# Two layers of cross-attention in float32: the projections of layer 0 in two column tiles of 64

## The chip, the cores and the metric

The kernel runs on one core of one Trainium2 chip. The metric is the device time of one execution in microseconds (us); of several runs the median is given. TensorE multiplies matrices and writes its results to PSUM, ScalarE and VectorE read PSUM and write SBUF, GpSimd works in SBUF, and SyncE issues most DMAs.

## The reference

The input x has 4 batches of 1024 rows of 512, the context 4 batches of 1024 rows of 384. Everything is float32. Layer 0 has 16 heads of 64, layer 1 has 16 heads of 32.

```python
def layer0(x, context):
    h = layernorm(x) * gamma + beta
    Q, K, V = h @ Wq, context @ Wk, context @ Wv          # 16 heads of 64: 1024 wide
    attn = softmax(Q K^T) * 64 ** -0.5                    # per head, 1024 x 1024
    return x + (attn V) @ Wo + bo

def layer1(x, context):
    xn = x * rsqrt(mean(x * x) + 1e-5) * norm_w
    q, (k, v) = xn @ wq, context @ wkv                    # 16 heads of 32: 512 wide
    q, k = normalised(rotated(q)), normalised(rotated(k)) # rotary, then length 1 per head
    attn = softmax(q k^T * sqrt(32))
    return x + (attn v) @ wout

out = layer1(layer0(x, context), context)
```

## The kernel before, in words

The work goes batch by batch; in each batch layer 0 comes first and layer 1 second. [...]

**Layer 0** works on pairs of heads (8 pairs of 2 x 64 = 128 features). The attention of a pair takes 8 steps, one for each 128 query rows (`Attention0.step`). A step does this:
- `scores` (L372): eight passes on TensorE, with 64 rows of the array for each of the two heads, so that two heads run side by side. The trace shows each float32 matmul as two passes.
- at every second step `factors_turned` (L440): two transposes of 128 x 128 (rT) bring the softmax's divisors to the layout of the product.
- VectorE takes each row's maximum (L395), ScalarE the exponential (L396), VectorE turns 32 x 32 squares over (L401), and at the end of every second step 16 DMAs (L407) put the squares of two steps where they belong (eT).
- part of the other work, up to 1.8 us by the program's own estimate, is issued behind the scores. The class `Units` keeps it as a list of small units with estimated costs, and `fill` issues units until the estimate is used up.
- at every second step `product` (L449), the product av with v: sixteen rounds of two column tiles of 64, one for each head.

The units of layer 0 are mostly projections: for the pair two ahead kT, qT and v (`project` and `values`, tiles pkT, pqT and pv), and the sums into x, which are the products with Wo of finished pairs (`add_units`, po, then added to x by VectorE at L301). Towards the end of layer 0 the first projections of layer 1 join them (`rotated_chains` and `value_chains`, k_p and pv from wkv), with transposes among them (L519, k_t). Between the layers there is a short stage with the last sums into x, the norm of layer 1 (transposes at L253), and the first q projections.

**Layer 1** works on blocks of four heads. Its scores (L597) use 32 rows of the array for each of four heads, and its products av (L636, L647) four column tiles of 32. The units there are projections of layer 1, sums into x, and the preparation of the next batch.

All projections and sums go through one helper, `matmul` (L158 is the call in it). It splits the columns of the stationary operand, that is the output's partitions, into `which["cols"]` column tiles and issues one matmul for each; the moving operand is the same for all of them. `which["cols"]` is read when a unit is issued. It is 1 at the start and in layer 0, 4 in layer 1, and is set back behind each batch's layer 1. Transposes do not go through the helper.

Of the kernel before, what the change touches and what calls it, by code (L numbers as in the profile page):

```python
# [107 lines left out]
def xattn_kernel(ctx: ExitStack, tc: tile.TileContext, a: dict, out: bass.AP):  # L108
# [10 lines left out]
    def score(name, shape=(P, S)):  # L119
        return ps_s.tile(list(shape), F32, tag="s", name=name)  # L120

    which = {"n": 0, "from": 0, "cols": 1}

    def bank(name):

# [13 lines left out]
    cols = const.tile([P, 3, NQ], F32, name="cols")  # L139
# [599 lines left out]
    for b in range(B):  # L739
# [6 lines left out]
        for p in range(NPAIR):  # L746
# [51 lines left out]
            for i in range(NT):  # L798
# [8 lines left out]
                n = NT * (NPAIR - p if later else 1) - i  # L807
# [41 lines left out]
        for half in range(2):  # L849
            n = 0  # L850
# [45 lines left out]
            kT, qT, v = kT1, qT1, att1.v1  # L896
        att1.finish()
        att1.quotient()
        which["from"], which["cols"] = 0, 1
        if b == B - 1:  # L900
            tail = flat(adds[1][6:])
        else:
# [42 lines left out]
```

## Time and profile before

| | |
|---|---|
| median of 3 runs | 2983.13 us (2977.34 to 2984.37) |
| profiled execution | 2979.04 us |
| its span, first to last instruction | 2976.8 us |
| granted TensorE clock | 0.997 |
| TensorE matmuls, weight loads | 2914.2 us busy, 1541.9 us busy |
| VectorE, ScalarE, GpSimd | 2228.5, 1429.5 and 416.5 us busy |

The profile is of one execution, so sums made from it are compared with that execution's time. Weight loads run beside matmuls on TensorE and are listed apart as PEld. In the groups of instructions a line gives the source line, engine, operation, the tiles written and read, the shape, the number of passes, the busy time, the mean time of one in ns, and the idle time of the engine before them with what ended it. The shape 128*64 means 128 rows and 64 columns of the array. The timeline gives the start, the length, and the number of passes of each stretch of equal instructions; the start of the next stretch tells how long the engine was taken, since the lengths shown include the time in which a result is still on its way. One batch takes about 737 us, of which 432 us lie between layer 0's first scores and its last.

### The profile page before, as it was taken

The numbers are of one execution on the slowest core, as the hardware profiler recorded it, in microseconds if no ns is written. First come the engines' busy times: TensorE is split into PE (matmuls) and PEld (weight loads), VectorE is DVE, ScalarE is ACT, GpSimd is POOL, SyncE is SP. The second block draws the span as 40 slices with busy tenths as digits, with TensorE's granted clock in tenths as the row PEclk, the third lists the DMA queues.
The fourth block names the chain that finished last, engine by engine and source line by source line (L and its number), as shares of the span: only waits on it lengthen the run. The fifth ranks groups of instructions, "written<-read, shape, count | busy, mean of one in ns | idle before, by whom it ended". The sixth has DMA issues, their size and how long they took to land.

```text
span 2976.8 us, 60525 instructions
## 1 busy us (share of the span) xinstructions
PE 2914.2 (98%) x24748; PEld 1541.9 (52%) x24748; DVE 2228.5 (75%) x2824; ACT 1429.5 (48%) x2265; POOL 416.5 (14%) x392
## 2 busy tenths in 40 slices
PE   8999999999999999999999999999999999999998
PEld 5544546555544555655554454555455455555544
DVE  4777795877777779587777777958767777795777
ACT  3444443656534444465644444446664444444664
POOL 0010012420000002232000000223100000023310
PEclk9999999999999999999999999999999999999999
DMA  5787674010388777301048887730104878772000
GB/s 146 169 197 180 158 178 114 21 35 25 74 200 196 183 161 178 95 21 35 25 95 213 183 177 169 166 84 21 35 25 117 209 176 182 167 171 66 2 2 30
DMA packets 177525, 348.49 MB, mean 117 GB/s; under 512 B 37600, under 2 KB 93152, under 8 KB 177248
## 3 DMA queue, kind: packets, MB, share of 16 engines
q1 hardware_dynamic: 175056, 343.43, 48.8%
q8 instruction: 196, 3.21, 0.5%
q10 hardware_dynamic: 2192, 1.19, 0.1%
q14 instruction: 81, 0.66, 0.1%
HBM read 67.64 MB, written 8.39 MB: 26 GB/s over the span
## 4 chain that ended last, share of the span: by engine, by line
PE 82%; DVE 8%; DMA 3%; SPq 3%; ACT 2%; issue 1%; POOL 1%; ACTq 0%; DVEq 0%
PE s L372 15%; PE av L449 13%; PE po L158 10%; PE s L597 7%; PE pv L158 7%; PE av L636 6%; PE pqT L158 6%; PE pkT L158 5%; PE q_p L158 3%; PE av L647 2%; SPq L407 2%; PE k_p L158 2%; DVE both L613 2%; DMA eT<-e 1%; PE rT L440 1%
## 5 line engine op out<-in xcount | busy, mean ns | idle before, releaser
L396 ACT ACTIVATE e<-s,m 128x1024 f32<-128x1024 f32 x512 | 565.6, 1109 | 666.7 <-DVE m L395 623.1
L395 DVE TENSOR_REDUCE m<-s 128x1 f32<-128x1024 f32 x512 | 602.6, 1218 | 321.4 <-PE s L372 321.4
L607 ACT ACTIVATE e<-s 128x1024 f32<-128x1024 f32 x512 | 496.5, 1022 | 315.3 <-PE s L597 300.2
L401 DVE STREAM_TRANSPOSE e<-e 128x1024 f32<-128x1024 f32 x512 | 606.6, 1223 | 46.9 <-ACT e L396 41.1
L372 PE MATMUL s<-qk 64*128 64x512 f32 x2048 | 520.5, 615 | 6.0 <-ACT e L396 5.3
L449 PE MATMUL av<-eT,v 128*64 128x256 f32 x4096 | 470.3, 382 | 7.8 <-DMA eT<-e 6.2
L613 DVE TENSOR_TENSOR both<-e 128x512 f32<-128x512 f32 x512 | 342.1, 699 | 128.9 <-ACT e L607 93.7
L449 PEld LDWEIGHTS av<-eT,v 128*64 128x64 f32 x4096 | 285.5, 137 | 205.3 <-issue 50.2
L372 PEld LDWEIGHTS s<-qk 64*128 64x128 f32 x2048 | 181.8, 186 | 262.6 <-issue 188.5
L597 PE MATMUL s<-q,k 32*128 32x256 f32 x4096 | 304.7, 401 | 5.8 <-ACT q L524 2.7
L597 PEld LDWEIGHTS s<-q,k 32*128 32x128 f32 x4096 | 190.8, 184 | 149.6 <-ACT e L607 71.4
L158 PE MATMUL po<-wo,vals 128*128 128x512 f32 x512 | 239.6, 601 | 2.5 <-ACT v L130 2.5
L158 PE MATMUL pqT<-hT,w 128*128 128x512 f32 (+1 forms) x800 | 241.3, 597 | 0.7 <-ACT hT L255 0.7
L441 ACT COPY vals<-rT 128x256 f32<-128x256 f32 x128 | 47.7, 372 | 327.4 <-PE rT L440 327.4
L301 DVE TENSOR_TENSOR x<-x,po 128x512 f32<-128x512 f32 x200 | 133.6, 678 | 82.6 <-PE po L158 82.6
L158 PEld LDWEIGHTS pv<-w,cT 128*128 128x128 f32 (+1 forms) x2400 | 176.7, 152 | 30.3 <-issue 27.2
L158 PE MATMUL pv<-w,cT 128*128 128x128 f32 (+1 forms) x2400 | 186.5, 275 | 0.0
L158 PE MATMUL pkT<-cT,w 128*128 128x512 f32 (+1 forms) x600 | 182.7, 601 | 1.0 <-ACT cT L130 1.0
L617 DVE TENSOR_TENSOR both<-both 128x1024 f32<-128x1024 f32 x128 | 159.7, 1248 | 4.4
L158 PEld LDWEIGHTS po<-wo,vals 128*128 128x128 f32 x512 | 90.9, 190 | 106.5 <-issue 102.3
L158 PEld LDWEIGHTS pqT<-hT,w 128*128 128x128 f32 (+1 forms) x800 | 85.9, 151 | 112.2 <-issue 105.9
L636 PE MATMUL av<-e,v 128*32 128x256 f32 x2048 | 137.0, 385 | 0.0
(461 smaller groups left out, 2669.9 us busy)
## 6 DMA issues: line engine op xcount, KB each, us to landing
eT<-e SPq DMA_DIRECT2D x2048, 128.0 KB, 2.4
xr<-in_x_dram SPq DMA_DIRECT2D x32, 256.0 KB, 4.0
x<-in_x_dram SPq DMA_DIRECT2D x32, 256.0 KB, 4.0
wo<-in_Wo_dram SPq DMA_DIRECT2D x16, 512.0 KB, 4.0
out_dram<-x SPq DMA_DIRECT2D x32, 256.0 KB, 2.7
w<-in_Wq_dram SPq DMA_DIRECT2D x31, 256.0 KB, 3.9
c<-in_ctx_dram SPq DMA_DIRECT2D x32, 192.0 KB, 3.8
wkv<-in_wkv_dram SPq DMA_DIRECT2D x16, 384.0 KB, 3.3
```

Source lines behind the costliest of these rows:

```text
L158: nc.tensor.matmul(o[rr], lhsT[:, rr], rhs, start=start, stop=stop)
L301: nc.vector.tensor_add(xt[t], xt[t], pp[0])
L372: nc.tensor.matmul(sc[j][:, kb * 512 : (kb + 1) * 512], pr["qT"][r[j], i * P : (i + 1) * P], pr["kT"][r[j], kb * 512 : (kb + 1) * 512], st ...
L395: nc.vector.tensor_reduce(m[:, j : j + 1], sc[j], AX.X, ALU.max, negate=True)
L396: nc.scalar.activation(e[j], sc[j].rearrange("p (g s) -> p g s", g=4), AF.Exp, bias=m[:, j : j + 1], accum_out=l[:, j : j + 1])
L401: nc.vector.transpose(e[j], e[j])
L449: nc.tensor.matmul(av[r[j], :W].rearrange("p (t a i) -> p t a i", t=BQ, a=4), pr["v"][:, k, r[j]], eT[:, j, :, :, k * 32 : (k + 1) * 32], ...
L597: nc.tensor.matmul(sc[j // 2][:, j % 2, c, :], kT[rr, g, k * P : (k + 1) * P], qT[rr, g, qb * WQ : (qb + 1) * WQ], start=True, stop=True,)
L607: nc.scalar.activation(e, sc[u], AF.Exp, scale=float(np.sqrt(np.float32(HD1))))
L613: nc.vector.tensor_add(self.both[:, kk, 2 * u : 2 * u + 2, :], es[u][:, :, 0, :], es[u][:, :, 1, :])
L617: nc.vector.tensor_add(self.both[:, 0], self.both[:, 0], self.both[:, kk])
L636: nc.tensor.matmul(self.av[rr, 0, :], v[g][:, 2 * kk + c, rr], es[j // 2][:, j % 2, c, :], start=first and c == 0, stop=end and c == 1,)
```

## The change

In layer 0 the helper splits every projection and every sum into x into two column tiles of 64, where it issued one matmul of 128 columns. In layer 1 it stays at four tiles. The order of the units, their estimated costs, the tiles, loads and evictions stay as they are.

```diff
@@ -119,7 +119,7 @@
-    which = {"n": 0, "from": 0, "cols": 1}
+    which = {"n": 0, "from": 0, "cols": 2}
@@ -896,7 +896,7 @@
         att1.finish()
         att1.quotient()
-        which["from"], which["cols"] = 0, 1
+        which["from"], which["cols"] = 0, 2
         if b == B - 1:
```

The helper itself is not edited:

```python
    def matmul(o, lhsT, rhs, start, stop):

        w = P // which["cols"]
        for j in range(which["cols"]):
            rr = slice(j * w, (j + 1) * w)
            nc.tensor.matmul(o[rr], lhsT[:, rr], rhs, start=start, stop=stop)
```

## The prediction

> **What bounds the kernel now.** I read the busy line first, then the groups of instructions by shape, then the timeline of TensorE alone, and last the starts of single matmuls in order.
>
> ```profile
> PE 2914.2 (98%) x24748; PEld 1541.9 (52%) x24748; DVE 2228.5 (75%) x2824; ACT 1429.5 (48%) x2265; POOL 416.5 (14%) x392
> ```
>
> TensorE is busy nearly all the time; no other engine comes near. Its groups by shape (stationary rows*columns; x counts passes, two to one f32 matmul):
>
> ```profile
> L449 PE MATMUL av<-eT,v 128*64 128x256 f32 x4096 | 470.3, 382 | 7.8 <-DMA eT<-e 6.2 <-DMA w<-in_Wq_dram 0.9 <-DMA x<-in_x_dram 0.7
> L158 PE MATMUL po<-wo,vals 128*128 128x512 f32 x512 | 239.6, 601 | 2.5 <-ACT v L130 2.5
> L158 PE MATMUL pqT<-hT,w 128*128 128x512 f32 x416 | 195.1, 601 | 0.0
> L158 PE MATMUL pv<-w,cT 128*128 128x128 f32 x1248 | 150.6, 277 | 0.0
> L158 PE MATMUL pv<-w,cT 128*32 128x128 f32 x1152 | 35.9, 273 | 0.0
> ```
>
> The 128*128 rows of L158 (3132 passes with the smaller ones) are what the change splits; the 128*32 row is the same work run in layer 1 in four column tiles. Idle time before these rows is a few us, so the length of layer 0 is the length of TensorE's own stream. Two steps of that stream, TensorE only:
>
> ```profile
> 1005.93 1.99 PE L372 MATMUL s<-qk 64*128 64x512 f32 x8
> 1007.85 0.44 PE L440 MATMUL rT<-ident,rb_(3, 3)_7795 128*128 128x128 f32 x2
> 1008.12 1.02 PE L158 MATMUL pkT<-cT,w 128*128 128x512 f32 x2
> 1009.07 3.67 PE L449 MATMUL av<-eT,v 128*64 128x256 f32 x32
> 1012.68 1.99 PE L372 MATMUL s<-qk 64*128 64x512 f32 x8
> 1014.60 2.84 PE L158 MATMUL pkT<-cT,w 128*128 128x512 f32 x6
> 1017.27 2.74 PE L158 MATMUL pqT<-hT,w 128*128 128x512 f32 x6
> ```
>
> Read start to start. A "round" is what runs side by side: one pass untiled, two passes of two tiles. The single starts give medians: a round of 512 takes 429 ns, of 256 takes 216, and both hold for 128*128, two tiles and four tiles alike. On top come two stalls wherever the shape of the tile changes:
> - at the boundary: 96 ns out of 128*128 (134 cases into scores, 106 into av), 103 out of 128*64, 99 out of 64*128, 117 out of 128*32;
> - in the first round after it, since the next load isn't ready: 107 ns into 128 columns, 54 into 64, 27 into 32 (58 for a 128-wide transpose[...]).
>
> So pkT x2 is 2 x 429 + 96 = 954 (0.95 read), av is 16 x 216 + 54 + 103 = 3613 (3.61), scores 4 x 429 + 107 + 99 = 1922 (1.92). Between transposes and untiled projections nothing is paid: rT takes 2 x 109 + 56.
>
> [...]
>
> **The change part by part.** Instruction order, loads, evictions, buffers and DMAs stay, so nothing is moved past a queue and no wait is added. What changes is the mode of L158 in layer 0, thus which boundaries pay. Counts are from the starts in order:
> 1. scores to projection, 124 times: 99 + 107 becomes 99 + 54, -53 each: -6.6 us. The boundary from 64*128 into 128*64 isn't in the trace; its neighbours are 99 (into 128*128) and 111 (32*128 into 128*32); I take 99, the other end adds 1.5.
> 2. projection to av, 106 times: 96 + 54 becomes 4, as between 128*32 projections and av in layer 1 (2 + 3): -146: -15.5 us.
> 3. av to projection, 5 times: 103 + 107 becomes 4: -1.0 us.
> 4. transpose to projection, 129 times (mostly rT, some k_t): 7 becomes 96 + 54, as the 22 times when rT goes straight to av: +143: +18.4 us.
> 5. projection to transpose, 19 times: 4 becomes 103 + 58: +3.0 us.
> 6. projection to scores, 134 times: 96 becomes 103: +0.9 us.
>
> Sum: -0.8 us. In the two steps above: with the transpose, scores to scores stays 6.75 us, for the switch only moves from behind the projection to ahead of it; in the other step 53 - 7 = 46 ns go. Odd-numbered steps are where something is won (123 x 46 ns = 5.7 us); transposes outside the pattern, in the stage between the layers and without av behind, give it back.
>
> 7. Rounds: 512 and 256 wide, nothing (429 and 216 in all tilings; 1 ns off would be 1 us). The 128-wide pv takes 111.7 ns a round untiled and 109.2 in four tiles; two tiles may be either: 1248 x 0 to 2.5 = 0 to -3.1 us. I take half, -1.5.
> 8. 3132 more passes and as many loads to issue: costed at nothing; streaming covers them. Four instructions a round of at least 109 ns are half of what the 128*32 pv issues in that time. If that cover goes, rival B.
>
> Total -2.3 us, of the profiled execution's 2979.04 us (span 2976.8, 2.2 around it). The median of the three runs, 2983.13, stands 4.1 above it, so on that footing 2980.8, say 2981. Nothing downstream must keep up: VectorE is at 75%, and TensorE's waits that remain in layer 0 (single ones of 0.4 to 1.8 us, mostly av waiting for eT) may swallow a few us of the 5.7 or be shortened by the switch that now lies ahead of them; I allow 3 us each way.
>
> **Rivals.**
> A, the forecast: stalls move and cancel, 2981, between 2976 and 2987 with the ends above. For it: every price but those of items 1 and 7 is read at the same shapes in this trace. Summing these prices and the single waits gives back the whole TensorE stream, 2968 us from first to last start, within 3 us.
>
> B, slower: two 64-column loads behind each other don't hide. av shows 54 in the round after a switch, but with 256-wide rounds and another moving operand for each tile. If a projection pays 107, as one 128-column load does, items 1 and 4 lose 53 in 253 places, 13.4 us: 2994, +0.4%. It decides from some 94 ns on. Instruction supply gives the same sign: 6264 more instructions are 24 blocks of the instruction queue's 16 KiB (196 packets now, 1.06 us median); were each waited for whole, 26 us: 3007. Against: four tiles pay 27, one load, not 107; and layer 1 runs 8 instructions in 216 ns. But in layer 0 the DMA engines are far busier.
>
> C, faster: the transposes cost less beside 64-column tiles than item 4 says, since the weight loads of the projection behind are already in when the two rT are done. All of item 4 gone would be -18.4: 2962. Half of it: 2972. Against: the 22 cases of rT to av pay 96 + 54 without exception. Or the waits for eT shrink: they hold about 8 us in front of av, so at most 2973.
>
> D: the change doesn't act, because a unit queued in layer 0 runs in layer 1. That is so already for the 128*32 rows, since the width is read when a unit is issued; the 3132 passes counted are those issued under the old width of one. I leave D no chance of note.
>
> **How the numbers follow.** A 0.68, B 0.12, C 0.20. About 0.3%, 9 us, is what a measurement of this kernel can tell from no change; the runs before lie 7 us apart. A falls almost wholly within it (0.65), with 0.02 on the faster and 0.01 on the slower side; B is slower for 0.11, C faster for 0.2. So faster 0.22, same 0.66, slower 0.12. The range, 2968 to 2990, takes A's ends, the scatter of medians and the milder half of C; B and the rest of C lie outside.
>
> **What would show it.** L158 with 128*64 x6264 and no 128*128 left. Item 1: projection behind scores has a first round of 429 + 54. Item 2: no stall between projection and av. Item 4: rT to projection 0.37 us where 0.27 stands, and 54 behind it. The step with rT unchanged at 6.75 us, the other 46 ns shorter. Wrong if a projection's plain round isn't 429, if its first round pays 107, if rT to projection stays at 0.27, or if waits for eT grow by over 5 us.

## The result, and the profile after

| | before | after |
|---|---|---|
| median of 6 runs | 2983.75 us (2977.34 to 2986.09) | 2969.19 us (2966.72 to 2972.11) |
| ratio | | 0.996, 95% interval 0.9947 to 0.9973 |
| profiled execution, its span | 2979.04, 2976.8 us | 2969.33, 2967.1 us |

The changed kernel is 0.4% faster, 12 us by the ratio, where 2 us were forecast. The busy line of the page after:

```profile
PE 2905.4 (98%) x27880; PEld 1454.7 (49%) x27880; DVE 2230.9 (75%) x2824; ACT 1430.4 (48%) x2265; POOL 417.2 (14%) x392
```

3132 passes more (27880 against 24748), TensorE busy as before. The groups of TensorE by shape, after:

```profile
L449 PE MATMUL av<-eT,v 128*64 128x256 f32 x4096 | 465.2, 380 | 7.3 <-DMA eT<-e 3.7 <-DMA x<-in_x_dram 3.2 <-issue 0.3
...
L158 PE MATMUL po<-wo,vals 128*64 128x512 f32 x1024 | 239.7, 599 | 3.0 <-ACT v L130 3.0
L158 PE MATMUL pqT<-hT,w 128*64 128x512 f32 x832 | 195.2, 600 | 0.0
L158 PE MATMUL pv<-w,cT 128*64 128x128 f32 x2496 | 147.5, 274 | 0.0
```

Twice the passes, the same busy time for po and pqT, 3.1 us less for pv, and 5.1 less for av, which no longer pays behind a projection: the last round ahead of it takes 429 ns where it took 522, its own first round 216 where it took 267. The timeline of TensorE over the two steps that the prediction shows, after (start, length, passes):

```profile
1000.59 1.99 PE L372 MATMUL s<-qk 64*128 64x512 f32 x8
1002.51 0.44 PE L440 MATMUL rT<-ident,rb_(3, 3)_8412 128*128 128x128 f32 x2
1002.88 1.08 PE L158 MATMUL pkT<-cT,w 128*64 128x512 f32 x4
1003.79 3.62 PE L449 MATMUL av<-eT,v 128*64 128x256 f32 x32
1007.34 1.99 PE L372 MATMUL s<-qk 64*128 64x512 f32 x8
1009.26 2.79 PE L158 MATMUL pkT<-cT,w 128*64 128x512 f32 x12
1011.88 2.74 PE L158 MATMUL pqT<-hT,w 128*64 128x512 f32 x12
1014.56 1.56 PE L372 MATMUL s<-qk 64*128 64x512 f32 x6
```

rT to projection is now 0.37 us, where 0.27 stood: the switch has moved there. Scores to scores is 6.75 us, as before. The other step goes from the scores at 1007.34 to those at 1014.56, so it takes 7.22 us where it took 7.26 (before, its scores start at 1012.68 and the next ones at 1019.94). Step by step the change does what the prices said. Where do the other us come from?

By stages, from the first to the last score of each layer, the two profiled executions differ so: layer 0 -6.8 us over the four batches, the stage between the layers +2.2 (0.54 in each batch, its transposes), **layer 1 -4.4**, where not one instruction was changed. The last is seen in the table by windows (columns: the stretch and its length; busy us and passes of PE, PEld, DVE, ACT, POOL; then granted clock, DMA share, GB/s). Before, at the seventh block of layer 1 in the second batch:

```profile
1361.00:1365.00 4.00, 1.79 (x32) 0.68 (x24) 3.96 (x8) 1.94 (x2) 0.56 (x1) 1.00 0.01 4
1365.00:1368.40 3.40, 3.39 (x30) 2.35 (x32) 2.84 (x4) 0.58 (x1) 3.26 (x2) 0.50 0.00 0
```

After, at the same place in the program:

```profile
1355.80:1359.80 4.00, 1.79 (x32) 0.68 (x24) 3.97 (x8) 1.94 (x2) 0.55 (x1) 1.00 0.00 0
1359.80:1363.20 3.40, 3.38 (x48) 1.78 (x48) 3.28 (x4) 0.59 (x1) 3.27 (x2) 1.00 0.02 5
```

In both TensorE idles 2.2 us for VectorE's sums. Before, the granted clock is then 0.50 for one stretch of 3.41 us (a half-clock window, as it is called below): a round 256 wide takes 427 ns where it takes 216, and 30 passes are done where 48 are done after. In these two profiles the kernel before met this in all four batches, the changed one in one. So the first question was chance or cause.

### The profile page after: what moved, and what is told of

It reads as the page before. It is cut to its first block, busy times and chain, and to the rows that moved or that the text cites. A ratio compares the mean times of both kernels' runs of the same rounds, so it can differ in the third digit from the quotient of the medians.

```text
span 2967.1 us, 66793 instructions
## 1 busy us (share of the span) xinstructions
PE 2905.4 (98%) x27880; PEld 1454.7 (49%) x27880; DVE 2230.9 (75%) x2824; ACT 1430.4 (48%) x2265; POOL 417.2 (14%) x392
## 4 chain that ended last, share of the span: by engine, by line
PE 85%; DVE 7%; DMA 2%; ACT 2%; SPq 1%; issue 1%; POOL 1%; DVEq 0%; ACTq 0%
PE s L372 16%; PE av L449 14%; PE po L158 11%; PE pv L158 8%; PE s L597 7%; PE pqT L158 7%; PE av L636 6%; PE pkT L158 5%; PE q_p L158 3%; PE av L647 2%; PE k_p L158 2%; DVE both L613 2%; PE rT L440 1%; DVE both L617 1%; SPq L407 1%
## 5 line engine op out<-in xcount | busy, mean ns | idle before, releaser
L449 PEld LDWEIGHTS av<-eT,v 128*64 128x64 f32 x4096 | 295.1, 137 | 186.2 <-issue 48.4
L158 PE MATMUL po<-wo,vals 128*64 128x512 f32 x1024 | 239.7, 599 | 3.0 <-ACT v L130 3.0
L158 PE MATMUL pqT<-hT,w 128*64 128x512 f32 (+1 forms) x1216 | 241.4, 598 | 0.7 <-ACT hT L255 0.7
L158 PEld LDWEIGHTS pv<-w,cT 128*64 128x64 f32 (+1 forms) x3648 | 168.5, 128 | 34.3 <-issue 31.2
L158 PE MATMUL pv<-w,cT 128*64 128x128 f32 (+1 forms) x3648 | 183.4, 274 | 0.0
L158 PE MATMUL pkT<-cT,w 128*64 128x512 f32 (+1 forms) x912 | 182.0, 601 | 0.9 <-ACT cT L130 0.9
L636 PE MATMUL av<-e,rest 128*32 128x256 f32 x2048 | 137.0, 385 | 0.0
L158 PE MATMUL q_p<-wq,hT 128*32 128x256 f32 (+1 forms) x1920 | 131.2, 380 | 0.0
```

What stands on the lines that cost most here:

```text
L158: nc.tensor.matmul(o[rr], lhsT[:, rr], rhs, start=start, stop=stop)
L449: nc.tensor.matmul(av[r[j], :W].rearrange("p (t a i) -> p t a i", t=BQ, a=4), pr["v"][:, k, r[j]], eT[:, j, :, :, k * 32 : (k + 1) * 32], ...
L636: nc.tensor.matmul(self.av[rr, 0, :], v[g][:, 2 * kk + c, rr], es[j // 2][:, j % 2, c, :], start=first and c == 0, stop=end and c == 1,)
```

## The experiments

The ratios are to the kernel before on the same chip, whose median was 2980.66 us (55 runs) in the first group, 2981.91 (28) in the second and 2980.87 (20) in the third.

### Both kernels once more

No edit. Theory 1: half-clock windows in layer 1 make up what the prices leave. Theory 2: the change itself shortens layer 1.

> The kernel before once more, unchanged. In the two profiles the changed kernel is 10 us shorter, of which the prices of the prediction (with 109.2 ns for a round of pv) explain 3.3. Theory 1: some 4 us of the rest lie in layer 1, where the change touches nothing: the kernel before had the half clock granted in four windows of 3.4 us there, the changed one in one; where such windows fall is a matter of the execution. Then this profile may show another number of half-clock windows inside the span than four, the time of its batches' layer 1 (259.5, 258.7, 258.8, 238.1 us before) differs by 1 to 2.5 us for each window that is gone or new, and layer 0 stays at 431.9 to 432.3 us in batches 1 to 3. Theory 2, the change shortened layer 1 by its work: this profile repeats layer 1 within 0.3 us and the four windows. Ratio 0.999 to 1.001 either way.

> The changed kernel once more. Both theories: 0.4% below the kernel before (0.994 to 0.998). Theory 1: layer 0 again 430.0 to 430.6 us in batches 1 to 3 (1.3 to 1.9 us under before), the stage between the layers 41.6 us (0.5 over before), and the number of half-clock windows not bound to be one. Theory 2: layer 1 again 257.2, 257.2, 258.1, 238.1 us.

Measured: before 0.9998 (0.9987 to 1.0009); after 0.9967 (0.9957 to 0.9976), 2970.67 us. The difference is real, about 10 us here where the first measurement gave 12. But the two new profiles have spans of 2971.4 and 2971.6 us: single executions scatter by more than the effect. Ahead of the very end the kernel before now had two half-clock windows and not four, with layer 1 at 259.8, 258.7, 257.3 and 236.5 us; the changed one had three, one of them in layer 0. The windows start at another phase from execution to execution: in the first two profiles their grid of 3.413 us stands 3.05 and 0.51 us behind the first instruction. So theory 2 falls. Layer 0 kept less still than I expected: 432.5, 429.8 and 430.6 us before, 430.0, 433.7 and 429.0 after. The 433.7 holds a wait for eT and a half-clock window behind it.

### A filler, at the wrong block

```diff
             if end:
+                if half == 0 and (qb, g) == (S // WQ - 1, 1):
+                    for j in [0, 1, 2, 3] * 5:
+                        rr = slice(j * HD1, (j + 1) * HD1)
+                        nc.tensor.matmul(
+                            self.av[rr, 1, :], v[g][:, 2 * kk, rr], es[j // 2][:, j % 2, 0, :], start=True, stop=True
+                        )
                 for i in (0, NT // 2 - 1):
```

> The kernel before with ten extra rounds of four column tiles (2.16 us of matmuls whose result is overwritten) in the idle 2.2 to 2.4 us in front of the last product of the first half of each batch's layer 1, where TensorE waits for VectorE's sums and behind which the half-clock windows lay. Theory 1: no half-clock window there any more, the rounds of pv behind it take 216 ns and not 427, layer 1 of batches 0 to 2 shrinks by 1.2 to 1.6 us each and of batch 3 by up to 1; in all 3 to 6 us, ratio 0.998 to 0.999. Theory 2: the filler lies in idle time and changes nothing, ratio 1.000, layer 1 as before.

> The changed kernel with the same filler. Theory 1: at most the one window in batch 3 goes, 0 to 1.5 us under the changed kernel, and against the filled kernel before what is left is the change's own part: 3 to 4 us by the prices, so a difference of 0.1 to 0.15% between the two filled ones. Theory 2: the two filled kernels differ by the whole 0.4% (12 us).

Measured: 1.002 (1.0012 to 1.0029) and 0.9996 (0.9986 to 1.0005). A miss, and my mistake: the idle stretches lie at the third and seventh block, the filler stood at the eighth, where TensorE has work. It serves as a control: 4 x 10 x 0.216 = 8.6 us more stream cost 6 us in the kernel before and 9 in the changed one. TensorE's stream is the time.

### The filler at the third and seventh block

```diff
-                if half == 0 and (qb, g) == (S // WQ - 1, 1):
-                    for j in [0, 1, 2, 3] * 5:
+                if half == 0 and (qb, g) in ((1, 0), (3, 0)):
+                    for j in [0, 1, 2, 3] * (4 if qb == 1 else 5):
```

> The first filler stood at the wrong block (the last of the half; TensorE's idle 1.7 and 2.4 us lie at the third and the seventh block). Here eight extra rounds (1.73 us) stand at the third and ten (2.16 us) at the seventh block's last product in each first half of layer 1, in the kernel before. Open is why the runs differ by 9.8 us (0.9967, 0.9957 to 0.9976) where the prices give 3.3. Theory 1, half-clock windows behind these idle stretches hit the kernel before more often: none is left there, the kernel gets 3 to 7 us faster than before (0.9977 to 0.999), and the changed one gains less. Theory 3, waits for transfers in layer 0: this kernel gains only what its own windows cost, 1 to 3 us on the mean, and so does the changed one. Theory 4, the fill costs as much as it saves: within 1 us of before.

> The changed kernel with the same filler at the third and seventh block. Theory 1: against the filled kernel before 3 to 4 us less (0.999), since the windows are gone from both. Theories 3 and 4: 9 to 10 us less (0.9965 to 0.997), as without filler.

Measured: 0.9975 (0.9964 to 0.9987), 2973.07 us, and 0.9964 (0.995 to 0.9978), 2971.37 us. 15.6 us of matmuls were added to the kernel before (18 rounds of 0.216 us in each batch), and it became 7 us faster by the ratio: the fill lies in idle time, and no half-clock window is left in layer 1 of either profile but at the very end of the last batch. The changed kernel gained 1 us (0.9967 without filler). The filled kernels stand 0.11 points apart where the unfilled ones stand 0.33 to 0.4. That is theory 1's number, but with intervals of 0.12 to 0.14 points each way it doesn't yet exclude 0.3.

### No product waits for a transfer

The other candidate: waits for eT in layer 0 (theory 3).

```diff
-                        eT[:, j, :, :, k * 32 : (k + 1) * 32],
+                        bo[:, :W].rearrange("p (t a i) -> p t a i", t=BQ, a=4),
```

> The kernel before, but the products av of layer 0 read a constant row (bo) in place of eT, so that no product waits for a transfer; the transfers are issued as before. The output is therefore another. Theory 3, waits for eT in layer 0 make up the 6 us that the prices leave: the 8 us of such waits in the profile go, and with them the half-clock windows behind the longest: 2968 to 2972 (0.996 to 0.997). Theory 1: 8 us of waits go as well, but the difference to the changed kernel in the same form stays 9 to 10 us.

> The changed kernel with the constant row in place of eT (its output is another too). Theory 3: 3 to 4 us under the kernel before in the same form, which is the change's price without waits. Theory 1: 9 to 10 us under it.

Measured: 0.997 (0.9962 to 0.9978) and 0.9937 (0.9922 to 0.9953), 2972.68 and 2962.53 us. Both gain, 9 and 8 us, and the difference stays 0.33 points, with some 0.17 of uncertainty each way. Theory 3 expected 0.10 to 0.13, and falls, if not by much. The profile of the kernel before in this form showed something new, a half clock within layer 0. Windows of that run:

```profile
1157.00:1167.30 10.30, 8.98 (x50) 4.22 (x47) 10.07 (x15) 5.00 (x10) 4.37 (x4) 1.00 0.89 216
1167.30:1174.10 6.80, 6.80 (x24) 2.82 (x23) 5.39 (x6) 2.67 (x5) 0.67 (x2) 0.50 0.64 146
```

It lasts two windows, 6.8 us, and came in three of the four batches. Layer 0 took 433.7 and 432.5 us in two of them against 429.3 in the one without, and 446.5 in the first batch, where 443.1 is usual: some 3 to 4 us each. Ahead of it the scores wait for ScalarE. The timeline of TensorE there, in the kernel before as first profiled:

```profile
1163.64 0.66 PE L519 MATMUL k_t<-ident,rot 128*128 128x128 f32 x4
1164.13 1.88 PE L158 MATMUL po<-wo,vals 128*128 128x512 f32 x4
1167.34 3.08 PE L372 MATMUL s<-qk 64*128 64x512 f32 x8 [1.32 <-ACT e L396]
```

and in the changed kernel:

```profile
1157.98 0.66 PE L519 MATMUL k_t<-ident,rot 128*128 128x128 f32 x4
1158.56 1.94 PE L158 MATMUL po<-wo,vals 128*64 128x512 f32 x8
1161.68 3.08 PE L372 MATMUL s<-qk 64*128 64x512 f32 x8 [1.18 <-ACT e L396]
```

The switch from the transpose puts po 0.09 us later behind k_t and its second round another 0.05; the scores can't start earlier anyway, so the idle stretch is 0.14 us shorter. I laid a window of 3.41 us over every place around it and took the share in which TensorE streams; scores of which only one head runs use half of the array's rows and count half. In batches without half clock there, the least share is 34% in all five profiles of the kernel before and its variants, and 38% in all five of the changed one and its variants. Of the real windows of layer 0 in these ten profiles, past the first 30 us, those in which TensorE streamed for 36% and less were followed by half clock, and none of 38% or more was. Hence theory 5: at this place only the kernel before can fall to half clock.

### All three stretches filled

```diff
+            if i == 0 and t == 3 and name in [f"po0_{b}_2" for b in range(B)]:
+                matmul(pp[0], lhs(cs[i])[:, t * P : (t + 1) * P], w(cs[i]), True, True)
             matmul(pp[0], lhs(cs[i])[:, t * P : (t + 1) * P], w(cs[i]), i == 0, i == n - 1)
```

on top of the filler at the third and seventh block.

> The kernel before with the filler at the third and seventh block of layer 1, and in each batch one extra matmul (0.86 us, overwritten) ahead of the sum into x in front of layer 0's step 2 of pair 7, where the scores wait 1.4 us for ScalarE. Theory 5: in any 3.41 us around that wait TensorE streams for at least 34% of the time before and at least 38% after the change (its sum starts 0.14 us later, behind the switch from the transpose), and half-clock windows come only behind some 35% or less: so the kernel before can fall to half clock there, for two windows and 3.3 us in each batch, at about a quarter of the phases of the clock's window, and the changed one cannot. With the stretches filled the kernel before gains 6 to 11 us (0.9963 to 0.998) and scatters less than without (runs within 8 us and not 16). The rival, the surplus lies elsewhere: 7 us as in the second filling (0.9975), no more.

> The changed kernel with the same three fillers. Theory 5: it gains only what layer 1's windows cost, 2 to 4 us under the changed kernel, and stands 2 to 5 us under the filled kernel before, near the price of 3.3. The rival: it stays 8 to 10 us under the filled kernel before.

Measured: **0.9968** (0.9956 to 0.9979), 2971.35 us, and **0.9965** (0.9953 to 0.9977), 2970.32 us. With its idle stretches filled, the kernel before is about as fast as the changed one: 0.03 points apart, 1 us, by the medians too. It gained 9.5 us; the changed one gained nothing that can be told. TensorE in the filled kernel before, same place:

```profile
1159.33 0.66 PE L521 MATMUL k_t<-ident,rot 128*128 128x128 f32 x4
1159.82 2.74 PE L158 MATMUL po<-wo,vals 128*128 128x512 f32 x6
1163.03 3.08 PE L374 MATMUL s<-qk 64*128 64x512 f32 x8 [0.47 <-ACT e L398]
```

Two passes more in po, 0.47 us of the wait left, and k_t to scores takes 3.70 us, as without the filler. The scatter shrank less than I expected: the runs lie within 9 us, not 16, though there are only 7 of them. Long waits for eT still bring single half-clock windows, one in this profile and two in the changed kernel's.

That the two come out level does not mean that the change is worth nothing by itself. Each run's granted clock is on record, and it splits the time: (1 - clock) x time is what half clock takes at most (less where TensorE waits anyway), and the rest is the time without it. An estimate from the means of these runs, in us:

| | runs before, changed | taken by half clock | the rest |
|---|---|---|---|
| both kernels once more | 55, 18 | 12.2, 6.9 | 2969.0, 2964.5 |
| third and seventh block filled | 10, 7 | 4.8, 5.1 | 2968.3, 2965.2 |
| all three stretches filled | 7, 5 | 3.0, 5.9 | 2969.3, 2965.3 |

Of the 9.7 us between the unedited kernels 5.3 are half clock (95% interval 1.4 each way) and 4.4 the rest (1.6 each way), near the prices. The rest keeps its difference when the stretches are filled, 3.0 and 4.0 us (2.0 and 2.8 each way); what goes is the half clock of the kernel before. The fully filled kernels are level because the five runs of the changed one had 3 us more of it.

### Divisors turned without the transpose mode

Item 4 of the prediction is its largest term, and it can be taken away: in place of the transposes, which are 128*128 passes in the traces, the helper issues plain matmuls with the identity in two column tiles of 64.

```diff
-                nc.tensor.transpose(rT[:, k * P : (k + 1) * P], self.rb[:, k, :], ident)
+                matmul(rT[:, k * P : (k + 1) * P], self.rb[:, k, :], ident, True, True)
```

> The changed kernel, and in layer 0 the divisors (rT) are turned by plain matmuls with the identity as the moving operand, in two column tiles of 64 through the helper, in place of transposes. Item 4 of the prediction says that the switch from rT to the projections gives back 143 ns 117 times, and rT to av 150 ns 22 times: with the prices of the trace this kernel is 19.5 us under the changed one (2950 to 2952, ratio to before 0.9895 to 0.991). If the cancelling was not the switch behind rT, it stays at the changed kernel's time.

Measured: 1.0005 (0.9997 to 1.0013), 2983.04 us, 12 us slower than the changed kernel where 19.5 us less were expected. The timeline of TensorE in that kernel, a step with rT:

```profile
1158.67 0.66 PE L158 MATMUL rT<-ident,rb_(6, 2)_9649 128*64 128x128 f32 x8
1159.16 1.03 PE L158 MATMUL k_p<-wkv,cT 128*64 128x256 f32 x8
1160.03 3.62 PE L449 MATMUL av<-eT,v 128*64 128x256 f32 x32
```

The switch is gone as item 4 says: from rT to what follows it 2 ns and 2 ns in the next round, median of 124 cases, where 96 and 54 stood. The trace has 102 of them into projections and 22 into av, not 117 and 22; with the 8 switches from a projection to rT that also go, the saving is still about 19 us. What I overlooked stands in the prediction's own lines: two transposes were x2, one pass each, and a float32 matmul takes two. rT now has four rounds of 109 ns and not two; 256 x 109 ns = 27.9 us more, less 19 to 19.5, is 8 to 9, against +12.4 by the medians (2970.67 for the changed kernel, measured on another chip). By the clocks 1 us of this is half clock; the remaining 2 to 3 us I did not trace.

### All transposes without the transpose mode

The same edit at L197, L253 and L519 too, with the three fillers.

> All transposes as plain matmuls through the helper, in two column tiles in layer 0 and in four in layer 1, with the three fillers on top. By the prices the switches around the transposes of both layers are worth 42.7 us against the changed kernel; the fillers 2 to 4 more: 2922 to 2927, ratio 0.980 to 0.982. If VectorE or ScalarE become the bound (75% and 48% busy now), part of it turns into waits of the scores for ScalarE, and it ends between 2927 and 2945.

Measured: 1.0075 (1.0063 to 1.0087), 3004.63 us. The same oversight, larger: 864 transposes x 109 ns = 94 us of passes for 43 us of switches. Of the 51 us that this leaves, 34 show against the filled changed kernel; where the rest went I did not trace. The page of this run:

```profile
PE 2971.6 (99%) x32344; PEld 1569.9 (52%) x32344; DVE 2235.3 (74%) x2824; ACT 1437.5 (48%) x2265; POOL 416.7 (14%) x392
```

No other engine became the bound. No version with the same output beats the changed kernel; those with fillers are level with it.

## Why the prediction was right, and where it was short

The measured 2969 us lie in the range (2968 to 2990) and on the side that it leaned to, but the likeliest case, 2981 and no change beyond 0.3%, was short by some 10 us. That the range held is partly luck: its lower end was put there for rival C, and nothing that rival C named came true.

1. **Items 1 to 6, the stalls that move: right.** In the starts of the changed kernel's passes, scores to projection pays 99 + 53 (124 times; the last round of the scores takes 526 ns, the first 512-wide one of the projection 480), projection to av 2 (429 and 216), transpose to projection 96 + 53 to 54 (202 and 480), projection to transpose 103 + 58 (530 and 165), projection to scores 103 + 107 (529 and 533). The boundary from 64*128 to 128*64, not shown before, is 99, the end that was taken. In the trace before, the weight load behind a first round starts 107 ns after that round where it goes into 128 columns (1014.70 against 1014.60 us) and 54 where it goes into 64, against 1 to 2 ns in plain rounds. (These prices are counted from 2 to 3 ns below the plain rounds of 429, 216 and 109 ns: 526 is 97 over 429 and stands as 99. So the prediction's three worked examples count 2 to 3 ns of each stall twice; in differences between the kernels this cancels.)
2. **Item 7, the rounds: the other end.** pv takes 109.2 ns a round, as in four tiles, so -3.1 us and not half of it. 512 and 256 wide are 429 and 216, unchanged.
3. **Item 8, nothing for issuing: right.** The instruction queue (q8) brought 220 packets of 16384 bytes where it brought 196, the 24 forecast, and rounds are no longer for it. The forecast can be worked out from the trace before: TensorE's 50139 instructions there are 256 for each packet. Rival B falls with this and with the 53 ns of item 1.
4. **The sum of the prices.** -0.8 - 3.1 = -3.9 us by the prediction's counts; boundary by boundary in the traces it is 3 to 4. Measured, with half clock taken off by the runs' clocks, it is 4.4 us between the unedited kernels (2.8 to 6.0).
5. **The step that failed: "I allow 3 us each way" for TensorE's remaining waits.** I took a wait to cost its own length. But where a wait left TensorE streaming for 36.3% or less of a window of 3413 ns, the next window ran at half the clock: 1.2 to 1.6 us on top at the seventh block (from the product that waited to the scores 3.80 us, where 2.45 are usual), 3 to 4 us for the pair of windows in layer 0. On the page only a clock of 0.997 hints at it; the table by windows shows it at once. The surplus over the prices, 6 to 9 us, is gone when the idle stretches are filled, and stays when the waits for eT are removed; by the clocks of the runs 5.3 us of the 6 in the repeat are half clock. So it is half clock behind idle stretches, and not transfers.
6. **Rival C named the right sign for a wrong reason.** Transposes don't cost less beside 64-column tiles (96 + 54 in all cases), and waits for eT were not the source.

What stays open is why the kernel before meets more half clock. Layer 0's stretch has a least share of 34% before and 38% after, on the two sides of the 36.3 to 37.5% between which the windows parted. In the first profile before, about a quarter of the phases fall on the low side there; this x 4 batches x 3.3 us gives an estimate of 3 to 4 us on the mean. By the clocks its filler saved 1.8 us (2.7 each way), and it was seen in one of five profiles. The filler in layer 1 took 7.4 us of half clock from the kernel before (2.7 each way) and 1.8 from the changed one (1.5 each way), so the larger part lies there, though layer 1 is the same in both, and at the seventh block a window has less than that at about half of the phases in either (1.5 to 2.0 of 3.41 us in the first two profiles). What may set them apart is the length of a batch. In the first profile the starts of layer 1 lie 736.7 to 737.4 us apart before, close to 216 windows of 3.413 us, so each batch met the clock's windows at nearly the phase that had just brought half clock. In the changed kernel's first profile two of them lie 733.8 and 734.4 us apart, close to 215 windows, and no half clock came; the third lies 735.3 us apart, and half clock came there. This fits, but no run tests it.

## What to carry to other kernels

Write down what TensorE pays at each change of tile shape, for the boundary and for the first round behind it, and count the boundaries before and after an edit; here a uniform shape saved 146 ns between projection and av, and where a 128*128 transpose stood ahead of the projection it cost 143. Stretches in which TensorE idled 1.3 us (layer 0) and 2.2 us (the seventh block) cost half-clock windows on top of their length, and redundant matmuls, in them and at the third block, were worth 9.5 us to the kernel before, about as much as the edit. Where such windows fall at random, as they did here, compare many runs and their mean granted clocks: two single profiles can hide the difference, as the second pair did with spans of 2971.4 and 2971.6 us.

## What the runs showed of the hardware that was not expected

- The granted clock fell to 0.5 in windows of 3413 ns on a grid that had another phase from execution to execution. In the first profile of the kernel before they start at 627.68, 1364.96, 2102.24 and 2839.52 us, 216.0 windows apart, and the next one, at 2969.23 us, 38.0 windows on; the changed kernel's first profile has 38.0 windows between its first two. No window without any work was needed: those in which TensorE streamed for up to a third of the time (24.7 to 31.3% in these two profiles) were enough.
- The share of streaming separates the windows of these traces without exception, if two things are minded: a round counts by the share of the array's 128 rows that it uses, not by its columns, and a transpose counts like a matmul. In the 14 profiles, past the first 30 us and up to the last scores, 30 full-clock windows had shares of 3 to 36.3%, and each was followed by half clock; 11934 had 37.5% or more, and none was. Were columns counted too, windows at the third block would have 26%, and yet they passed; counted by rows the least share there is 37.5%, so its filler was not needed. At half clock, three windows that were busy 62 to 65% were followed by another such window, and thirty with 84% or more were not.
- At layer 0's stretch the half clock lasted two windows (6827 ns in three batches): the first of them was one of the three just named, since the waits behind the slowed stream grew too (the scores there took 4.19 us where they take 3.08).
- A float32 transpose of 128 x 128 was one pass of 109 ns in these traces (two of them are rT x2); a matmul with the identity of that size was two rounds of 109 ns (two of them, in two column tiles, are rT x8).
